# A graph attention kernel: one chunk of source rows in every eighth quad is loaded row by row by SyncE, and node inputs are loaded at the start of a quad's sums

## Chip, cores and metric

The kernel runs on one core of one Trainium2 chip. The metric is the device time of one execution in microseconds; the time before is the median of three runs. Five engines work side by side and wait for each other through semaphores: TensorE (PE, its weight loads PEld), VectorE (DVE), ScalarE (ACT), GpSimd (POOL) and SyncE (SP). SyncE computes nothing here; its instruction queue issues most DMAs. Gathers, which read one table row per index, are issued by GpSimd.

## What is computed

One layer of graph attention over 12,500 nodes and 200,000 edges, the edges sorted by destination, added to its input:

```python
h = jnp.maximum(_layernorm(x, axis=-1), 0.0)
h = (h @ W_node.T).reshape(num_nodes, H, HD)           # H = 4 heads of HD = 32
e = (edge_features @ W_edge.T).reshape(num_edges, H, HD)
att = jnp.sum(jnp.concatenate([h[src], h[tgt], e], -1) * a, axis=-1)
att = jnp.where(att > 0, att, 0.2 * att)
m = jnp.maximum(segment_max(att, tgt), 0.0)
ex = jnp.exp(att - m[tgt])
denom = segment_sum(ex, tgt) + (num_edges - deg)[:, None] * jnp.exp(-m)
out = x + segment_sum((ex / denom[tgt])[:, :, None] * h[src], tgt)
```

(The function is written here with the same names and fewer lines.) What costs time is `h[src]`: for every edge the row of its source node must be fetched, in no order.

## The kernel before

**Tiling.** The edges are cut into 392 groups of 511 (`G`, `NE`; a 512th place carries the sum of the group before). A group is four chunks of 128 edges (`J = 4`, one edge per partition). Four groups make a quad (`QG = 4`), so there are 98 quads. Two to four quads make a softmax batch (`supers`; four in the middle).

**Node stage** (lines 307 to 448). Normalized nodes are multiplied by the weights; rows of 137 float32 (548 bytes: values, a count and the source's share of the logit) are stored to the DRAM tensor `table`, target shares to `side`. Meanwhile the first gathers fetch raw inputs.

**Edge stage** (lines 463 to 895). The program is in an order written out by hand (`manual_schedule`): each engine gets its instructions in the order in which the Python code issues them; `together` interleaves generators step by step. For quad q:

- `fetch(q)`: SyncE loads edge features `ea` and destinations `db` (`fetch_edges`, lines 302 and 304) and, in `fetch_windows`, a window of target shares `pw` and one of node inputs `xw` for each group (lines 502 and 505). The windows' addresses are loaded into SyncE's registers first (`windows`, line 486). GpSimd issues the quad's 16 gathers from `table` into the buffer `ga` (line 141), which holds eight quads (`QUADS`). `fetch(q + 2)` is called when the logits of q begin.
- `logits(q, i)` for each group: VectorE compares destinations with node numbers (`at`, line 536), TensorE multiplies (lines 542 and 545); `add_sources` (lines 557 and 559) adds the sources' share out of `ga`.
- `softmax(s)` for a batch: transposes, scans (lines 592 to 661).
- `sums(q)`: VectorE weighs the gathered rows (line 736) and makes the marks `hot` (line 749); TensorE sums (line 754). `complete_group` carries the last row of the group before into the next (lines 683 and 687), makes the last product (line 688) and copies the sums to `pt` (line 689). A group's slot in `ga` is free for another quad's gathers once these products are done.
- `divide(q)`: VectorE divides (line 776), adds the node input `xw` (line 780), and SyncE stores the four windows of results to `out` (line 783). Neighbouring windows overlap, so a store waits until the one before has landed.

In SyncE's queue an iteration in the middle reads: `ea`, `db`, `pw` four times, `xw` four times, four stores. `db` has two buffers, so its load waits until VectorE has read the older one. All of SyncE's DMAs share eight completion semaphores in turn; a DMA waits until the one eight places before it has landed.

Of the kernel before, what the change touches and what calls it, by code (L numbers as in the profile page):

```python
# [8 lines left out]
F32 = mybir.dt.float32  # L9
BF16 = mybir.dt.bfloat16  # L10
I32 = mybir.dt.int32
AF = mybir.ActivationFunctionType
OP = mybir.AluOpType
AX = mybir.AxisListType

P = 128
H, HD = 4, 32
HW = HD + 1
D = H * HD
# [5 lines left out]
R_CNT, R_SRC, ROW = H * HW, H * HW + 1, H * HW + 5  # L25

J = 4
GE = J * P
NE = GE - 1
WIN = 96  # L30
SPAN = 92
QG = 4
# [4 lines left out]
AT_ONCE = 4  # L37
RAW, MORE = 4, 2
QUADS = 8
SETS = max(NODE_T, QG * J)  # L40
PAD = 1 << 20

# [6 lines left out]
def kernel(  # L49
# [35 lines left out]
    nc = tc.nc  # L85
# [8 lines left out]
    table = dram.tile([NP, ROW], F32, name="table")  # L94
# [27 lines left out]
    quads = blocks(G, QG)  # L122
    nq = len(quads)
# [4 lines left out]

    ga_all = consts.tile([P, QUADS, QG, J, ROW], F32, name="ga")
    GA, GATHERED = {}, set()  # L130

    def gather(q, rows, width, lo, hi):

        g0, m = quads[q]
        ga = GA[q] = ga_all[:, q % QUADS]
        for i in range(lo, hi):
            n = -(-min(E - (g0 + i) * NE + 1, GE) // P)
            if n < J:
                nc.vector.memset(ga[:, i, n:, :], 0.0)
            for j in range(n):  # L140
                nc.gpsimd.indirect_dma_start(  # L141
                    out=ga[:, i, j, 0:width], out_offset=None, in_=rows,
                    in_offset=bass.IndirectOffsetOnAxis(ap=srci[:, g0 + i, j:j + 1], axis=0))

    def held_gather(q, i, rows, width):

        nc.vector.memset(ga_all[0:1, q % QUADS, i, 0, 0:1], 0.0)
        gather(q, rows, width, i, i + 1)
# [8 lines left out]
    with tc.manual_schedule():  # L157
# [6 lines left out]
        for _ in range(AT_ONCE):  # L164
            q, i = early.pop(0)
# [12 lines left out]
        with tc.tile_pool(name="prep", bufs=1) as prep, tc.tile_pool(  # L178
            name="prep_ps", bufs=1, space=bass.MemoryType.PSUM
# [21 lines left out]
        def statistics(pool, rows, T):  # L201


            assert nc.vector.BN_STATS_DIM == 6
            stats = pool.tile([P, SETS, 6], F32, name="stats")
            for t in range(T):
# [3 lines left out]
            two = stats[:, :T, :].rearrange("p t (o k) -> p t o k", k=3)  # L210
            both = pool.tile([P, SETS, 2], F32, name="both")
            nc.vector.tensor_tensor(both[:, :T, :], two[:, :, 0, 1:3], two[:, :, 1, 1:3], op=OP.add)
            apart = pool.tile([P, SETS], F32, name="apart")
            nc.vector.tensor_tensor(apart[:, :T], two[:, :, 0, 1], two[:, :, 1, 1], op=OP.subtract)
# [92 lines left out]
        with tc.tile_pool(name="node", bufs=2) as node, tc.tile_pool(  # L307
            name="node_ps", bufs=2, space=bass.MemoryType.PSUM
        ) as node_ps, tc.tile_pool(name="index", bufs=1) as index, tc.tile_pool(
            name="index_ps", bufs=1, space=bass.MemoryType.PSUM  # L310
# [152 lines left out]
    with tc.tile_pool(name="work", bufs=2) as work, \  # L463
            tc.tile_pool(name="turned", bufs=1) as turned, \
            tc.tile_pool(name="ps", bufs=1, space=bass.MemoryType.PSUM) as ps:
        XW, LG, AT, U, DR = {}, {}, {}, {}, {}
# [17 lines left out]
        def windows(of, size, g, n):  # L484

            return nc.values_load_multi_w_load_instructions(
                of[0:1, g:g + n], engines=[mybir.EngineType.SP], min_val=0, max_val=(N - 1) * size,
                skip_runtime_bounds_check_because="a destination's row, and that is a node")[1]

        as_bytes = lambda d: d.bitcast(U8)  # L490
        rows_at = lambda d, at, size, rows=SPAN: as_bytes(d.rearrange("n c -> (n c)"))[
            bass.ds(at, rows * size)].rearrange("(n c) -> n c", c=size)
# [3 lines left out]
        def fetch_windows(q):  # L496
            g0, m = quads[q]
            pw = PW[q] = load.tile([SPAN, QG, SIDE], BF16, name="pw")
            xw = XW[q] = work.tile([WIN, QG, D], F32, name="xw", bufs=8)
            at = windows(base_side, 2 * SIDE, g0, m)  # L500
            for i in range(m):
                nc.sync.dma_start(as_bytes(pw[:, i, :]), rows_at(side, at[i], 2 * SIDE))
            at = windows(base_row, 4 * D, g0, m)
            for i in range(m):
                nc.sync.dma_start(as_bytes(xw[0:moved(q), i, :]), rows_at(x, at[i], 4 * D, moved(q)))
# [15 lines left out]
        def open_logits(q):  # L521
            if q == supers[of_quad[q]][0]:
                fetch_rows(of_quad[q])
            if q + 2 < nq:
                fetch(q + 2)
            AT[q] = work.tile([SPAN, QG, GE], BF16, name="at")
            LG[q] = ps.tile([P, QG, J, PIECES, H], F32, name="lg")
# [188 lines left out]

        def sums(q):

            g0, m = quads[q]
            s = of_quad[q]  # L720
            s0, sm = groups(s)
            ga = GA.pop(q)
            heads = lambda t: t[:, :, 0:sm * H].rearrange("p j (h g) -> p j h g", h=H)
            ex, xs, facs = XS[s]
            fc = facs[WIN:WIN + 1, 0:sm * H].rearrange("p (h g) -> p h g", h=H)
            pt = work.tile([WIN + 1, QG, ROW], F32, name="pt", bufs=3)
            hot = HOT.pop(q) if q in HOT else marks(q)
            beside = xs[:, :, 0:sm * (H + 1)].rearrange("p j (h g) -> p g j h", g=sm)
            nc.scalar.copy(ga[:, :m, :, R_CNT:R_SRC + H], beside[:, g0 - s0:g0 - s0 + m])

            def weigh(i):

                if i < m:
                    val = ga[:, i, :, 0:H * HW].rearrange("p j (h w) -> p j h w", w=HW)
                    weight = heads(ex)[:, :, :, g0 + i - s0]
                    nc.vector.tensor_tensor(  # L736
                        val, val, weight.unsqueeze(3).to_broadcast([P, J, H, HW]), op=OP.mult)

            ahead = 1 if q >= nq - 2 else 0
            for i in range(ahead):  # L740
                weigh(i)
            for i in range(m):
                g = g0 + i
                if q == nq - 1 - FREE and i == 1:
                    for k in range(FREE):
                        HOT[nq - FREE + k] = marks(nq - FREE + k)
                weigh(i + ahead)
                if q < nq - FREE:
                    nc.vector.tensor_tensor(  # L749
                        hot[:, i, :, 0:WIN], lane_ps.unsqueeze(1).to_broadcast([P, J, WIN]),  # L750
                        slot[:, g, :].unsqueeze(2).to_broadcast([P, J, WIN]), op=OP.is_equal)
                acc = ps.tile([P, 512], F32, name="acc", bufs=3)[0:WIN + 1, 0:ROW]
                for j in range(1, J):
                    nc.tensor.matmul(acc, hot[:, i, j, :], ga[:, i, j, :], start=j == 1, stop=False)  # L754
                complete()
                begun.append((q, i, ga, hot, pt, acc, fc[:, :, g - s0]))
                yield

        def divide(q, pt, den, lo, hi):

            n, R = hi - lo, moved(q)
            xw = XW[q][0:R, lo:hi]
            pt = pt[0:R, lo:hi]
            den = den[:, lo:hi]
            others = work.tile([WIN, QG], F32, name="others")[0:R]
            nc.vector.tensor_scalar(others[:, :n], pt[:, :, R_CNT], -1.0, float(E),
                                    op0=OP.mult, op1=OP.add)
            nc.vector.tensor_tensor(den, den, others[:, :n].unsqueeze(2).to_broadcast([R, n, H]),
                                    op=OP.mult)
            val = pt[:, :, 0:H * HW].rearrange("p g (h w) -> p g h w", w=HW)  # L770
            nc.vector.tensor_tensor(den, den, val[:, :, :, HD], op=OP.add)
            nc.vector.reciprocal(share_ps[0:R, :n, :], den)  # L772
            if not lo:
                RES[q] = work.tile([WIN, QG, D], F32, name="res")[0:R]
            res = RES[q][:, lo:hi]
            nc.vector.tensor_tensor(  # L776
                res[:, :n, :].rearrange("p g (h d) -> p g h d", d=HD), val[:, :, :, 0:HD],
                share_ps[0:R, :n, :].unsqueeze(3).to_broadcast([R, n, H, HD]), op=OP.mult)
            add = nc.gpsimd if q == nq - 2 or q == nq - 3 and lo else nc.vector
            add.tensor_tensor(res[:, :n, :], res[:, :n, :], xw, op=OP.add)  # L780
            at = windows(base_row, 4 * D, quads[q][0] + lo, n)
            for i in range(n):
                nc.sync.dma_start(rows_at(out, at[i], 4 * D, R), as_bytes(res[:, i, :]))

        def all_logits(q):
            flush()
            open_logits(q)
            for i in range(QG):
                logits(q, i)
                yield  # L790
            state["logits"] = q
# [51 lines left out]
        with tc.manual_schedule():  # L843
# [4 lines left out]

            held = [(q, i) for q in range(raw, min(QUADS, nq)) for i in range(raws(q), quads[q][1])]
            GATHERED.update(range(raw, QUADS))  # L850

# [241 lines left out]
```

## Time and profile before

| what | value |
|---|---|
| median of three runs | 2580.49 us (2579.14 to 2584.17) |
| the profiled execution | 2560.06 us, span of its instructions 2558.3 us |
| TensorE busy | 1425.0 us (56%) |
| VectorE busy | 1370.2 us (54%) |
| ScalarE busy | 403.5 us (16%) |
| GpSimd busy | 1507.2 us (59%) |
| mean granted TensorE clock | 0.526 |
| DMA | 297 MB in 195,917 packets, 116 GB/s |

The busy time of an engine is the union of its instructions; issuing a DMA, waiting and register work are not counted, so SyncE has no row. GpSimd's instruction for a gather counts as busy while it writes the transfer's descriptors; the data move afterwards. "Remote" as a releaser means that the profile saw the semaphore change but no instruction whose end fits the time of the change. The end of a matmul is modelled.

### The profile page before, as it was taken

How to read it: one execution, taken by the hardware profiler on the slowest of the kernel's cores; microseconds unless marked ns; L12 is line 12 of the kernel's file. 1: busy time of each engine (PE TensorE's matmuls, PEld its weight loads, DVE VectorE, ACT ScalarE, POOL GpSimd, SP SyncE). 2: the span in 40 equal slices, each digit the busy share in tenths (PEclk: the TensorE clock that was granted, in tenths of full speed). 3: DMA queues.
4: the chain of work that ended last, by engine and by line, in shares of the span. 5: the costliest groups of instructions: out<-in, count | busy, mean ns of one | idle time of the engine just before them, and what ended most of it. 6: DMA issues, size and time to landing. Idle time of an engine off the chain costs nothing. (4 is left out here: it accounts for less than half of the span.)

```text
span 2558.3 us, 27296 instructions
## 1 busy us (share of the span) xinstructions
PE 1425.0 (56%) x7317; PEld 1265.1 (49%) x7317; DVE 1370.2 (54%) x3362; ACT 403.5 (16%) x1531; POOL 1507.2 (59%) x1609
## 2 busy tenths in 40 slices
PE   4555645555555555555555555555655655655486
PEld 3544545544544445445545544544544544544475
DVE  4543545554554555555555555554554554555587
ACT  4533211111111111111111111111111110111112
POOL 6445546566666666566666666666666666666602
PEclk9665655555555555555555555555555555555556
DMA  5433354444445454444444444444444444434330
GB/s 181 153 111 97 99 133 122 109 119 125 113 119 129 108 132 121 106 125 117 117 125 117 116 124 117 116 121 121 116 120 112 123 114 120 123 100 119 94 94 17
DMA packets 195917, 297.27 MB, mean 116 GB/s; under 512 B 70633, under 2 KB 143593, under 8 KB 186354
## 3 DMA queue, kind: packets, MB, share of 16 engines
q1 hardware_dynamic: 143952, 183.30, 26.2%
q0 software_dynamic: 50112, 109.61, 17.4%
q10 hardware_dynamic: 1698, 2.58, 0.3%
q8 instruction: 61, 1.00, 0.2%
q14 instruction: 94, 0.77, 0.1%
HBM read 269.63 MB, written 25.73 MB: 115 GB/s over the span
## 5 line engine op out<-in xcount | busy, mean ns | idle before, releaser
L141 POOL DMA_INDIRECT ga<-table,srci x1494 | 1418.7, 950 | 903.9 <-issue 400.2
L754 PE MATMUL acc<-ga,hot 128*97 128x137 f32 x2352 | 647.6, 447 | 263.6 <-ACT hot L709 100.5
L754 PEld LDWEIGHTS acc<-ga,hot 128*97 128x97 f32 x2352 | 515.9, 278 | 287.3 <-ACT hot L709 101.9
L683 DVE TENSOR_TENSOR ga<-acc,facs 1x132 f32<-1x132 f32 x391 | 115.9, 296 | 710.7 <-ACT pt L689 597.9
L688 PE MATMUL acc<-ga,hot 128*97 128x137 f32 x784 | 267.7, 444 | 361.0 <-ACT ga L687 315.8
L545 PE MATMUL lg<-wblk,ea 128*128 128x8 f32 x1568 | 409.4, 359 | 0.0
L688 PEld LDWEIGHTS acc<-ga,hot 128*97 128x97 f32 x784 | 188.4, 277 | 396.7 <-ACT ga L687 342.3
L545 PEld LDWEIGHTS lg<-wblk,ea 128*128 128x128 f32 x1568 | 381.8, 309 | 0.0
L689 ACT COPY pt<-acc 97x137 f32<-97x137 f32 x392 | 107.1, 273 | 1529.1 <-remote 942.1
L542 PEld LDWEIGHTS <-at 92*128 92x128 bf16 x1568 | 213.9, 165 | 231.5 <-DVE at L536 95.8
L736 DVE TENSOR_TENSOR ga<-ga,ex_ps 128x528 f32<-128x528 f32 x392 | 268.7, 686 | 28.0 <-remote 27.7
L536 DVE TENSOR_TENSOR at<-const_ps,db 92x512 bf16<-92x512 f32 x392 | 267.3, 683 | 5.8
L542 PE MATMUL lg<-pw,at 92*128 92x12 bf16 x1568 | 170.6, 182 | 166.5 <-DVE at L536 80.1
L749 DVE TENSOR_TENSOR hot<-const_ps,slot 128x384 f32<-128x384 f32 x384 | 209.2, 545 | 0.0
L646 PE MATMUL ex_ps<-ident,ex 64*128 64x64 f32 (+2 forms) x112 | 18.6, 315 | 164.0 <-ACT ex L635 99.8
L646 PEld LDWEIGHTS ex_ps<-ident,ex 64*128 64x128 f32 (+2 forms) x112 | 13.8, 208 | 167.1 <-ACT ex L635 102.1
L141 POOL DMA_INDIRECT ga<-in_x_dram,srci x72 | 68.6, 952 | 43.6 <-issue 20.2
L687 ACT COPY ga<-acc 1x1 f32<-1x1 f32 x391 | 59.9, 153 | 189.5 <-DVE ga L683 113.7
L557 DVE TENSOR_REDUCE st<-lg 128x64 f32<-128x192 f32 x98 | 35.0, 357 | 87.9 <-remote 37.6
L395 PE MATMUL row_ps<-wcat,hT 128*128 128x137 f32 x198 | 45.7, 389 | 52.1 <-issue 15.6
L776 DVE TENSOR_TENSOR res<-pt,const_ps 92x512 f32<-92x512 f32 (+3 forms) x102 | 67.5, 662 | 4.4 <-issue 0.6
L780 DVE TENSOR_TENSOR res<-res,xw 92x512 f32<-92x512 f32 (+2 forms) x99 | 67.4, 681 | 3.4
(137 smaller groups left out, 1067.6 us busy)
## 6 DMA issues: line engine op xcount, KB each, us to landing
db<-in_dst_dram SPq DMA_DIRECT2D x98, 768.0 KB
ea<-in_edge_t_dram SPq DMA_DIRECT2D x98, 512.0 KB
ga<-table,srci POOLq DMA_INDIRECT x1494
xw<-in_x_dram SPq DMA_DIRECT2D x384, 46.0 KB
out_dram<-res SPq DMA_DIRECT2D x384, 46.0 KB
pw<-side SPq DMA_DIRECT2D x392, 2.2 KB
table<-row SPq DMA_DIRECT2D x9, 616.5 KB
xt<-in_x_dram SPq DMA_DIRECT2D x9, 576.0 KB
```

Of the source, the lines that this page charges most:

```text
L141: nc.gpsimd.indirect_dma_start(out=ga[:, i, j, 0:width], out_offset=None, in_=rows, in_offset=bass.IndirectOffsetOnAxis(ap=srci[:, g0 + i, ...
L536: nc.vector.tensor_tensor(at[:, i, :], node_ps[0:SPAN, g0 + i:g0 + i + 1].to_broadcast([SPAN, GE]), db[0:SPAN, i, :], op=OP.is_equal)
L542: nc.tensor.matmul(lg[:, i, j].rearrange("p k h -> p (k h)"), at[:, i, j * P:(j + 1) * P], sw, start=i + j == 0, stop=False, skip_group_ch ...
L545: nc.tensor.matmul(lg[:, i, 2 * w:2 * w + 2, 0, :], ea[:, i, w, :], wblk, start=False, stop=True, skip_group_check=True)
L683: nc.vector.tensor_tensor(ga[0:1, i, 0, 0:H * HW].rearrange("p (h w) -> p h w", w=HW), before[WIN:WIN + 1, 0:H * HW].rearrange("p (h w) -> ...
L688: nc.tensor.matmul(acc, hot[:, i, 0, :], ga[:, i, 0, :], start=False, stop=True)
L689: nc.scalar.copy(pt[:, i, :], acc)
L736: nc.vector.tensor_tensor(val, val, weight.unsqueeze(3).to_broadcast([P, J, H, HW]), op=OP.mult)
L749: nc.vector.tensor_tensor(hot[:, i, :, 0:WIN], lane_ps.unsqueeze(1).to_broadcast([P, J, WIN]), slot[:, g, :].unsqueeze(2).to_broadcast([P, ...
L754: nc.tensor.matmul(acc, hot[:, i, j, :], ga[:, i, j, :], start=j == 1, stop=False)
L776: nc.vector.tensor_tensor(res[:, :n, :].rearrange("p g (h d) -> p g h d", d=HD), val[:, :, :, 0:HD], share_ps[0:R, :n, :].unsqueeze(3).to_ ...
L780: add.tensor_tensor(res[:, :n, :], res[:, :n, :], xw, op=OP.add)
```

## The change

In 11 quads (16, 24, 32 … 96) the last chunk of the last group is no longer gathered: the loop over chunks in `gather` runs one step less. Its 128 rows are loaded by SyncE, each by a DMA of 548 bytes into a tile `rows`, with 16 row addresses at a time read into registers. The generator `by_rows` issues four of these DMAs at each step, and `divide` takes one step after each store. When the logits of such a quad begin, ScalarE copies `rows` into the quad's place in `ga`. The indices come by a small DMA and are turned into byte offsets by one VectorE instruction for each such quad. Apart from this, `xw` is loaded in a function of its own, `fetch_inputs`, called at the start of `sums(q)`, where it was loaded with `pw`, and has three buffers instead of eight.

```diff
+AHEAD, EVERY = 16, 8
...
+    whole = lambda g: E - g * NE + 1 >= GE
+    BY_ROW = {q: QG - 1 for q in range(AHEAD, nq, EVERY)
+              if quads[q][1] == QG and whole(quads[q][0] + QG - 1)}
...
-            for j in range(n):
+            for j in range(n - (q in BY_ROW and i == BY_ROW[q])):
                 nc.gpsimd.indirect_dma_start(
...
         def fetch_windows(q):
             g0, m = quads[q]
             pw = PW[q] = load.tile([SPAN, QG, SIDE], BF16, name="pw")
-            xw = XW[q] = work.tile([WIN, QG, D], F32, name="xw", bufs=8)
             at = windows(base_side, 2 * SIDE, g0, m)
             for i in range(m):
                 nc.sync.dma_start(as_bytes(pw[:, i, :]), rows_at(side, at[i], 2 * SIDE))
+
+        def fetch_inputs(q):
+            g0, m = quads[q]
+            xw = XW[q] = work.tile([WIN, QG, D], F32, name="xw", bufs=3)
             at = windows(base_row, 4 * D, g0, m)
             for i in range(m):
                 nc.sync.dma_start(as_bytes(xw[0:moved(q), i, :]), rows_at(x, at[i], 4 * D, moved(q)))
...
         def sums(q):
 
+            fetch_inputs(q)
             g0, m = quads[q]
...
+        def by_rows():
+
+            prepared = []
+
+            def prepare(q):
+                g = quads[q][0] + BY_ROW[q]
+                of = work.tile([1, P], I32, name="of")
+                nc.sync.dma_start(of, src.rearrange("(o e) -> o e", o=1)[
+                    :, (g + 1) * GE - P:(g + 1) * GE])
+                return of
+
+            nodes = sorted(BY_ROW)
+            of = prepare(nodes[0])
+            yield 0
+            for k, q in enumerate(nodes):
+                at_row = work.tile([1, P], I32, name="at_row")
+                nc.vector.tensor_scalar(at_row, of, float(4 * ROW), None, op0=OP.mult)
+                rows = ROWS[q] = work.tile([P, ROW], F32, name="rows")
+                for p0 in range(0, P, QG * QG):
+                    if p0 == P // 2 and k + 1 < len(nodes):
+                        of = prepare(nodes[k + 1])
+                    at = windows(at_row, 4 * ROW, p0, QG * QG)
+                    for p in range(QG * QG):
+                        nc.sync.dma_start(as_bytes(rows[p0 + p:p0 + p + 1, :]),
+                                          rows_at(table, at[p], 4 * ROW, 1))
+                        if p % QG == QG - 1:
+                            yield 0
+
+        ROWS, row_steps = {}, by_rows()
+        next(row_steps)
...
                 nc.sync.dma_start(rows_at(out, at[i], 4 * D, R), as_bytes(res[:, i, :]))
+                next(row_steps, None)
 
         def all_logits(q):
             flush()
             open_logits(q)
+            if q in BY_ROW:
+                nc.scalar.copy(GA[q][:, BY_ROW[q], J - 1, :], ROWS.pop(q))
```

## The prediction

> **What bounds the kernel now.** I read the page's groups first, then the time-ordered instructions of GpSimd, ScalarE and TensorE, then SyncE's waits. A group line shows count and shapes, then busy us and mean ns, then idle us before it and what ended it.
>
> ```profile
> L141 POOL DMA_INDIRECT ga<-table,srci x1494 | 1418.7, 950 | 903.9 <-issue 400.2 <-remote 258.2 <-PE acc L688 162.9
> L689 ACT COPY pt<-acc 97x137 f32<-97x137 f32 x392 | 107.1, 273 | 1529.1 <-remote 942.1
> ```
>
> No engine is over 59% busy, so shares decide nothing. The gathers idle 400 us in 0.30 us steps between neighbours (1.25 us from one to the next) and some 420 us waiting for TensorE to free a buffer. That last looks as if TensorE, not GpSimd, were the limit. The order of time says otherwise (start us, duration us, idle before and releaser in brackets):
>
> ```profile
> 1248.23 0.94 POOL L141 DMA_INDIRECT ga<-table,srci  x1 [2.46 <-remote]
> 1249.47 0.94 POOL L141 DMA_INDIRECT ga<-table,srci  x1 [0.30 <-issue]
> ...
> 1261.96 0.94 POOL L141 DMA_INDIRECT ga<-table,srci  x1 [0.30 <-issue]
> 1265.63 0.94 POOL L141 DMA_INDIRECT ga<-table,srci  x1 [2.73 <-remote]
> ```
>
> ```profile
> 1257.66 0.78 PE L688 MATMUL acc<-ga,hot 128*97 128x137 f32 x2 [0.30 <-issue]
> 1266.24 0.77 PE L688 MATMUL acc<-ga,hot 128*97 128x137 f32 x2 [5.29 <-ACT ga L687]
> ```
>
> ```profile
> 1257.45 0.15 ACT L687 COPY ga<-acc 1x1 f32<-1x1 f32 x1 [0.36 <-issue]
> 1265.40 0.27 ACT L689 COPY pt<-acc 97x137 f32<-97x137 f32 x1 [7.79 <-remote]
> ```
>
> GpSimd runs twelve gathers, three groups, then stops. TensorE finished a group's sum at 1258.44; the copy waiting for it began at 1265.40, only 2.5 us after GpSimd's run ended at 1262.90. The next group's L688 stood behind that copy. So TensorE's signal reaches nobody while gathers run, and everything moves on after GpSimd has stopped for want of a buffer. The pattern repeats: run starts at 1345.00, 1362.40, 1379.68, 1396.93, 1414.45, 1424.12, 1441.46. Sixteen groups take 96.5 us: 64 gathers at 1.25 us (80 us) and six pauses of 2.4 to 5.0 us. The pauses follow the runs, so the rate is GpSimd's.
>
> The second witness is the end, where the gathers are over (last start 2435.4). The chain of waits has:
>
> ```profile
> 2451.60 1.18 DVE run L601
> 2485.17 1.18 DVE run L601
> ```
>
> That is one softmax to the next, two quads: 16.8 us a quad, although these short softmax batches cost more per quad than the middle's batches of four. With gathers a quad takes 96.5/4 = 24.1 us. The consumers could go faster; GpSimd's runs hold them.
>
> SyncE is the queue that gets the work. Its waits (us in all, times, longest):
>
> ```profile
> SPq L304 <- DVE at L536: 394.4, 44, 22.2
> SPq L783 <- DMA out_dram<-res: 218.2, 164, 2.8
> ```
>
> and a stretch of its queue:
>
> ```profile
> 1247.90 6.04 SPq L783 DMA_DIRECT2D out_dram<-res  x4
> 1254.04 0.38 SPq L302 DMA_DIRECT2D ea<-in_edge_t_dram  x1
> 1266.74 0.34 SPq L304 DMA_DIRECT2D db<-in_dst_dram  x1
> ...
> 1271.28 4.94 SPq L505 DMA_DIRECT2D xw<-in_x_dram  x4
> ...
> 1317.52 1.40 SPq L505 DMA_DIRECT2D xw<-in_x_dram  x4
> ```
>
> SyncE idles before `db`, and between the stores of one quad, each waiting for the one before to land. Its issues come at two paces: the same four take 1.40 us or 4.94 us (0.35 or 1.24 each), the latter late in a gather run.
>
> **The change, part by part.**
>
> *Eleven gathers go* (quads 16, 24 … 96; GpSimd's stream falls from 1494 to 1483). Each is 0.945 + 0.30 = 1.25 us. Where do they fall? Counting gathers in the trace, quad 48's last starts at 1256.96: eighth of the run 1248.23 to 1262.90, which then ends in a 2.73 us pause. Ten of the eleven stand like that, four before a pause called remote; quad 40's has eight behind it. So the run is eleven long, GpSimd stops 1.25 us earlier, and by the reading above the signal and all after it come 1.25 us earlier. 11 x 1.25 = 13.7 us off the path. Bounds: 0, if the pause only grows; and 11 x 24.1/16 = 16.6, if pauses shrink with the gathers. I take 13.7: the pauses show as fixed (2.36 to 2.73 after runs of twelve).
>
> *SyncE gets 1408 one-row loads of 548 bytes*, 16 per quad over 88 quads, four behind each store; 88 register loads, 11 index loads. At the short pace a row takes 0.35 us, four 1.4 us. The stores above start (6.04 - 0.25)/3 = 1.93 us apart, of which about 0.38 is work: 1.55 us of waiting, in which four rows hide. Three of four sets hide; the last (1.4 us) and a register load about every quad (0.5 us) do not: 1.9 us a quad. The cover is the `db` idle: 394 + 75 (the wait ended by DVE `col`) + 23 over 98 quads = 5.0 us a quad. Cost taken: 0. Without any cover it would be 88 x 1.9 = 167 us. At the long pace the four take 5 us, so one set in four at that pace adds about (5.0 - 1.6) = 3.4 us a quad; 5.3 against 5.0 is near the edge, but the next item gives some back, and a delay is not at once a loss: quad 48's `db` went out at 1266.74 and its first reader, L536, ran at 1292.8, and other quads show 25 to 38 us. What is issued late is `ea`, `db`, `pw` and the stores; their readers L536 and L542 come an iteration later, and `res` has two buffers.
>
> *Node inputs move* from behind `pw`, where four issues took 4.94, 4.97, 1.40 and 4.19 us in successive quads, to the start of the quad's sums, right behind the previous stores and rows. No DMA is added; at the short pace it is 1.4 us plus the register load. That returns up to 2.5 us of SyncE time a quad, off the path. New is a wait: the add L780 now needs `xw` loaded about one iteration (some 20 us) before, formerly many. Behind L780 on VectorE stand the next L536, L736 and L749, and TensorE behind them. A load issued within 15 us is in time. Cost 0; if SyncE falls behind by an iteration it is the saturation rival.
>
> *Copies and indices.* Eleven ScalarE copies of 128x137: between L729 (128x80, 0.33) and L661 (128x256, 0.37), so 0.35 each, 3.9 us in all; ScalarE is 16% busy and waits before L689 (942 us). They wait for eight DMA lanes, whose last row was stored behind a quad two iterations earlier; L594, L687 and L689 queue behind. Eleven VectorE multiplications of 1x128 at most 0.30 (L683, 1x132): 3.3 us, right behind a finished `res`. Taken as 0, together at most 7 us.
>
> *The tail.* Quad 97's `xw` is now issued between the last stores, about 1.9 us of SyncE. Before, L780 of that quad ran at 2548.5 and the store ahead at 2543.25, so it lands with a microsecond to spare: 0.5 us.
>
> Sum: -13.7 + 0.5 = -13.2. On the profiled span of 2558.3 (execution 2560.06) that gives 2545. The runs' median is 20.4 us above that execution; I subtract the same: 2580.5 - 13.2 = 2567.
>
> The Trainium skill (DMA: Bandwidth & Descriptors, Rules for kernel authors) speaks against this change: many small transfers should be merged, since below 64 KB one pays mostly overhead. If every row cost a landing, as a chained store does here, the result is the saturation rival below. The four `xw` issues in 1.40 us show independent loads not waiting for each other.
>
> **Rivals.**
>
> *SyncE saturates (slower).* Place: rows behind stores, at the long pace. SyncE has 5.0 us of `db` idle and 3 x 1.55 = 4.6 us between stores, 9.6 us a quad; 16 rows and 0.5 of register load use it up at 0.57 us a row. From there on each 0.1 us a row costs 1.6 us x 88 = 141 us. At 0.63 us (one row in three at the long pace): 0.06 x 16 x 88 = 84, less 13: 2651. If all waited for landings, 1.93 a row: 1.36 x 16 x 88 = 1915 more. For: the long pace exists and begins near these DMAs. Against: `xw` leaves it, and stores mostly come just after the release.
>
> *The pauses lengthen (slower).* The added issues and completions travel where TensorE's signals are stuck, and a pause grows by one row set's share, say the 0.35 us of one issue per quad: 88 x 0.35 = 31, so 2598. For: SyncE and TensorE are held up together. Against: 1408 packets beside 143,952 of that queue are 1%.
>
> *No gain.* The consumers need the time anyway, the pause grows by what GpSimd saves: 2580. For: GpSimd is released by TensorE. Against: 16.8 us a quad without gathers.
>
> *It doesn't do what it says:* excluded, the emitted order shows 1483 gathers.
>
> **How the numbers follow.** Forecast (2562 to 2571) 0.60; pauses lengthen 0.15; SyncE saturates 0.13; no gain 0.12. Predicted 2567. Its own range 2560 to 2573. For eight in ten: down to 2555 (16.6 saved, and some runs' spread, 2579 to 2584), up to 2606, which takes in no gain and most of the lengthened pauses and leaves saturation out. This kernel's measurement tells about 0.2% (5 us) from no change. Faster 0.61 (forecast and a sliver), same 0.12, slower 0.27.
>
> **What would show it.** Right: runs of eleven gathers in quads 16, 24 …, the pause behind them still 2.4 to 2.7 us, two softmax batches there in about 191.7 us, not 193; `db` idle smaller but present; L780 without a DMA wait. Wrong: `db` idle gone and `ea` late for L545; L780 released by `xw`; L689's remote idle up by as much as GpSimd saved.

## The result and the profile after

| | before | after |
|---|---|---|
| median | 2577.7 us (6 runs, 2570.57 to 2584.17) | 2691.01 us (6 runs, 2680.74 to 2718.28) |
| ratio, 95% interval | | 1.0455, 1.04 to 1.0511 |
| profiled execution | 2560.06 us, span 2558.3 | 2718.28 us, span 2716.5 |

The kernel became 113 us slower by the medians; 2567 had been forecast, with a range up to 2606. The profiled execution of the changed kernel is the longest of its six, so single sums of its trace are 1% large; the two traces lie 158 us apart, not 113.

The groups of the changed kernel, in the columns of the prediction's first fence (the add of node inputs, L780 before, is now L819; it had sat idle 3.4 us in all):

```profile
L145 POOL DMA_INDIRECT ga<-table,srci x1483 | 1417.3, 956 | 1054.8 <-issue 401.8
...
L696 ACT COPY pt<-acc 97x137 f32<-97x137 f32 x392 | 107.4, 274 | 1313.1 <-remote 723.2
...
L819 DVE TENSOR_TENSOR res<-res,xw 92x512 f32<-92x512 f32 (+2 forms) x99 | 67.1, 677 | 346.9 <-DMA xw<-in_x_dram 317.5
```

Eleven gathers are gone, yet GpSimd idles 151 us more than before (903.9). ScalarE's copy waits less for "remote" than before (942.1). The new wait is the third line. The waits of all engines say what GpSimd waits for (us in all, times, longest):

```profile
POOL ga L145 <- PE acc L695: 372.1, 75, 23.7
...
DVE res L819 <- DMA xw<-in_x_dram: 317.5, 58, 12.3
...
POOL ga L145 <- remote: 193.5, 87, 3.4
```

The same two waits of GpSimd were 162.9 us (36 times) and 260.3 us (105 times) before. The remote pauses have not lengthened: 2.22 us each against 2.48. What grew is waiting for a real product that comes late. Counting a run of gathers as ended by a gap of more than 0.6 us, 107 runs had 12 gathers and 14 had 8 before; now 39 have 12 and 103 have 8.

SyncE's own waits:

```profile
SPq L308 <- DVE at L543: 73.6, 11, 22.4
SPq L822 <- DMA out_dram<-res: 71.3, 74, 3.8
```

Before, these were 394.4 and 218.2 us. The idle time that was to cover the rows is used up: from the start of `ea`'s issue to the start of `db`'s was 7.79 us on the mean over the 98 quads before, and is 1.63 now. A stretch of SyncE's queue (start us, us from the first issue's start to the last one's end, line, transfer, count):

```profile
1302.12 0.32 SPq L822 DMA_DIRECT2D out_dram<-res  x1
1303.79 1.67 SPq L790 DMA_DIRECT2D rows<-table  x4
1306.44 0.29 SPq L822 DMA_DIRECT2D out_dram<-res  x1
1307.12 3.62 SPq L790 DMA_DIRECT2D rows<-table  x4
1310.83 0.62 SPq L822 DMA_DIRECT2D out_dram<-res  x1
1312.27 6.41 SPq L790 DMA_DIRECT2D rows<-table  x4
1319.38 0.01 SPq L822 DMA_DIRECT2D out_dram<-res  x1
1319.48 1.19 SPq L790 DMA_DIRECT2D rows<-table  x4
1321.41 1.41 SPq L512 DMA_DIRECT2D xw<-in_x_dram  x4
1322.91 0.37 SPq L306 DMA_DIRECT2D ea<-in_edge_t_dram  x1
1323.38 0.37 SPq L308 DMA_DIRECT2D db<-in_dst_dram  x1
```

The first and last of the four stores begin 17.3 us apart; over all quads in the middle the median is 14.2 us, before 5.9. Only then can `xw` go out, at 1321.41, and `db` follows `ea` at once. What comes of it, in the order of time, first on VectorE, then TensorE, then GpSimd (in brackets the idle time before and its releaser):

```profile
1320.66 0.68 DVE L815 TENSOR_TENSOR res<-pt,const_ps 92x512 f32<-92x512 f32 x1 [7.57 <-DMA rows<-table]
1327.28 0.69 DVE L819 TENSOR_TENSOR res<-res,xw 92x512 f32<-92x512 f32 x1 [5.94 <-DMA xw<-in_x_dram]
...
1328.03 0.67 DVE L543 TENSOR_TENSOR at<-const_ps,db 92x512 bf16<-92x512 f32 x1
```

```profile
1328.75 0.22 PE L549 MATMUL lg<-pw,at 92*128 92x12 bf16 x2 [15.63 <-DVE at L543]
...
1331.31 0.66 PE L695 MATMUL acc<-ga,hot 128*97 128x137 f32 x2
```

```profile
1323.63 0.94 POOL L145 DMA_INDIRECT ga<-table,srci  x1 [0.30 <-issue]
1332.24 0.95 POOL L145 DMA_INDIRECT ga<-table,srci  x1 [7.67 <-PE acc L695]
```

This is one chain: the add stands 5.94 us for `xw`, the comparison L543 runs only behind it in VectorE's order, TensorE has stood 15.63 us for that comparison, the group's last product L695 ends at 1331.97, and GpSimd goes on 0.27 us later after 7.67 us without work. (L815's releaser is named as a row load; that instruction waits for four semaphores, and the `res` it writes is freed by stores. The name is the profile's inference.)

The end is as it was. The chain of waits has two scans of the softmax 33.56 us apart, as before:

```profile
2607.55 1.18 DVE run L608
...
2641.11 1.18 DVE run L608
```

From the last gather's start to the end of the span it was 122.9 us and is 125.2 us. The loss lies in the middle.

### The profile page after: what moved, and what is told of

It is laid out like the page before. It is cut to its first block, busy times and chain, and to the rows that moved or that the text cites. A ratio compares the mean times of both kernels' runs of the same rounds, so it can differ in the third digit from the quotient of the medians.

```text
span 2716.5 us, 30468 instructions
## 1 busy us (share of the span) xinstructions
PE 1405.4 (52%) x7317; PEld 1265.4 (47%) x7317; DVE 1370.6 (50%) x3373; ACT 408.7 (15%) x1542; POOL 1506.3 (55%) x1598
## 5 line engine op out<-in xcount | busy, mean ns | idle before, releaser
L549 PEld LDWEIGHTS <-at 92*128 92x128 bf16 x1568 | 220.1, 167 | 603.6 <-DVE at L543 446.4
L695 PE MATMUL acc<-ga,hot 128*97 128x137 f32 x784 | 263.4, 439 | 205.7 <-ACT ga L694 136.5
L695 PEld LDWEIGHTS acc<-ga,hot 128*97 128x97 f32 x784 | 192.7, 279 | 226.5 <-ACT ga L694 147.7
L543 DVE TENSOR_TENSOR at<-const_ps,db 92x512 bf16<-92x512 f32 x392 | 267.2, 682 | 6.0
L819 DVE TENSOR_TENSOR res<-res,xw 92x512 f32<-92x512 f32 (+2 forms) x99 | 67.1, 677 | 346.9 <-DMA xw<-in_x_dram 317.5
L815 DVE TENSOR_TENSOR res<-pt,const_ps 92x512 f32<-92x512 f32 (+3 forms) x102 | 67.5, 662 | 82.6 <-DMA out_dram<-res 42.5
L399 PEld LDWEIGHTS row_ps<-wcat,hT 128*128 128x128 f32 x198 | 37.1, 266 | 67.7 <-ACT hn L233 28.6
L663 PE MATMUL acc<-ident,run 64*128 64x64 f32 (+2 forms) x112 | 18.8, 317 | 90.7 <-ACT facs L660 73.7
```

Source lines behind the costliest of these rows:

```text
L399: nc.tensor.matmul(row_ps[:, t, :ROW], hT[:, t, :], wcat, start=True, stop=True)
L543: nc.vector.tensor_tensor(at[:, i, :], node_ps[0:SPAN, g0 + i:g0 + i + 1].to_broadcast([SPAN, GE]), db[0:SPAN, i, :], op=OP.is_equal)
L549: nc.tensor.matmul(lg[:, i, j].rearrange("p k h -> p (k h)"), at[:, i, j * P:(j + 1) * P], sw, start=i + j == 0, stop=False, skip_group_ch ...
L695: nc.tensor.matmul(acc, hot[:, i, 0, :], ga[:, i, 0, :], start=False, stop=True)
L815: nc.vector.tensor_tensor(res[:, :n, :].rearrange("p g (h d) -> p g h d", d=HD), val[:, :, :, 0:HD], share_ps[0:R, :n, :].unsqueeze(3).to_ ...
```

## Experiments

The runs were made on three chips, and each ratio is against runs of the kernel before on the same chip. Before took 2017.86 us on the first (7 runs), 2577.77 us on the second (17) and 2557.69 us on the third (17); the second and third are of the kind on which the change was first measured. Differences in us are worked out from the ratios. In the expectations, theory S is that SyncE's time to issue sets the pace (the saturation rival), rival L is that inputs loaded late do the harm, and rival P that the pauses of the gathers lengthen; other letters are told where they are used.

### First chip: parts of the change alone

**Inputs late, no rows, all gathers.**

```diff
-    BY_ROW = {q: QG - 1 for q in range(AHEAD, nq, EVERY) ...}
+    BY_ROW = {}
-        ROWS, row_steps = {}, by_rows()
-        next(row_steps)
+        ROWS, row_steps = {}, iter(())
```

> Only the move of the node inputs: loaded at the start of the sums with three buffers, all gathers kept, no rows. Theory S (SyncE's issuing time now sets the pace, because of the rows): no change, 2578 within 0.5%, db idle on SyncE still 4 to 5 us a quad. Rival L (the inputs come too late and hold VectorE at the add): a good part of the 113 us shows here too, 2620 or more, with waits of the add on the load of xw.

2027.96 us, ratio 1.005 (1.0033 to 1.0067). The moved inputs cost 10 us on this chip, a tenth of what the change costs on the other. The add did wait for `xw`, 102.9 us in 31 pieces, so L's wait exists here without any row; the same kernel on the third chip, below, shows no such wait.

**Rows, inputs early** (`fetch_inputs` called in `fetch`, eight buffers; to make room, rows and their addresses share a tile with `node_at`).

```diff
-    node_at = consts.tile([P, G], F32, name="node_at")
+    node_all = consts.tile([P, 2 * ROW + 2 * P], F32, name="node_at")
+    node_at = node_all[:, 0:G]
...
-            xw = XW[q] = work.tile([WIN, QG, D], F32, name="xw", bufs=3)
+            xw = XW[q] = work.tile([WIN, QG, D], F32, name="xw", bufs=8)
...
             fetch_windows(q)
+            fetch_inputs(q)
...
-            fetch_inputs(q)
             g0, m = quads[q]
             s = of_quad[q]
...
-                of = work.tile([1, P], I32, name="of")
+                k = nodes.index(q) % 2
+                of = node_all[0:1, 2 * ROW + k * P:2 * ROW + (k + 1) * P].bitcast(I32)
...
-                at_row = work.tile([1, P], I32, name="at_row")
+                at_row = of
-                rows = ROWS[q] = work.tile([P, ROW], F32, name="rows")
+                rows = ROWS[q] = node_all[:, k % 2 * ROW:(k % 2 + 1) * ROW]
```

> Rows by SyncE and eleven gathers fewer, but the inputs loaded two quads ahead with eight buffers as before the change. S: SyncE has as much to issue as in the changed kernel, so about as slow, 2660 to 2700, and something else than xw is late (db, ea, pw or res). L: the harm is gone, 2564 to 2578. Rival P (rows lengthen GpSimd's pauses): slow, but with idle time of SyncE before db left.

2209.83 us, ratio 1.0951 (1.0921 to 1.098). With the inputs early the loss is not gone, so L is not the whole of it. But this kernel turned out to be no clean copy of the change, as its instructions by line show (count, then ns: least, median, most, then first and last start in us):

```profile
L791 SPq MOVE node_at<-table x1408: 29/29/37, 172.8 to 2073.1; - x176
L791 SPq DMA_DIRECT2D node_at<-table x1408: 227/228/332, 172.9 to 2073.1; - x176
```

```profile
L491 SPq TENSOR_LOAD <-base_row x200: 278/572/947, 101.1 to 2200.9; - x100
...
L491 SPq TENSOR_LOAD <-node_at x88: 3436/3536/3699, 169.3 to 2062.7; - x88
```

The rows are quick here (0.34 us from one to the next), and the register load of 16 addresses takes 3.54 us; in the changed kernel's trace it took 1.24. Eighty-eight times 2.3 us are 202 us, about as much as this kernel lost (192 us). So its size says nothing of the change's, and an aligned version follows on the second chip. What is late here are the divisions: by the profile VectorE waited 274.9 us for stores and 252.2 us for row loads before L816. SyncE also has less idle time on this chip: from the start of `ea`'s issue to that of `db`'s it was 2.89 us a quad in the first experiment, and is 0.90 here.

**No rows, eleven gathers fewer, inputs early** (ScalarE copies ones in place of rows, so the sums of 11 chunks are not the reference's).

```diff
-        ROWS, row_steps = {}, by_rows()
-        next(row_steps)
+        ROWS, row_steps = {q: ones[:, 0:1].to_broadcast([P, ROW]) for q in BY_ROW}, iter(())
```

(and `fetch_inputs` in `fetch` with eight buffers, as above)

> Eleven gathers fewer and no rows loaded: the place in ga gets ones by the same ScalarE copy, inputs early as before the change; the sums of 11 chunks are therefore not the reference's. All theories share the prediction's first term: 11 x 1.25 = 13.7 us less, 2564. If GpSimd's rate does not set the pace: 2578.

2006.23 us, ratio 0.9938 (0.9922 to 0.9955): -12.5 us. The gathers' term stands, -13.7 forecast.

**Rows loaded and not used, all gathers kept, inputs early.**

```diff
-            for j in range(n - (q in BY_ROW and i == BY_ROW[q])):
+            for j in range(n):
...
-            if q in BY_ROW:
-                nc.scalar.copy(GA[q][:, BY_ROW[q], J - 1, :], ROWS.pop(q))
```

(the rest as in the second kernel)

> Rows loaded by SyncE but not used, all gathers kept, inputs early: the cost of the 1408 loads by themselves. S: as e2, at most 14 us more, 2660 to 2715. L: no change, 2578. P: as e2 plus 14 us, SyncE not saturated.

2208.07 us, ratio 1.0941 (1.0911 to 1.0971), the same as with eleven gathers fewer. The loss needs neither the copy nor the missing gathers, and where SyncE is the bound the gathers saved do not show.

### Second chip: the change itself, aligned, halved, without addresses

**The changed kernel as it is.**

> The changed kernel as it is, beside the versions with early inputs and on whatever chip these four share. Theory S (SyncE's issue time is the bound): the ratio to before stays above 1.03; SyncE's register loads of 16 addresses show 1.24 us as in the first trace of this kernel and rows 0.34 us apart where the chip does not hold them back. Rival A (the harm of +9.5% in e2 and e5 came from their own register loads, 3.54 us each instead of 1.24, because the address tile lay at 1096 bytes, not at a multiple of 64): if this chip is like that of the first four experiments, this kernel is far below theirs, within about 1% of before. Rival C (the +4.5% belongs to the chip of the first pair, where signals are held back and rows go 0.75 us apart): ratio 1.00 to 1.01 on a chip where before takes 2018 us, 1.045 on one where it takes 2578 us.

2689.78 us, ratio 1.0431 (1.0413 to 1.0449), as in the first pair, and as S and C both had it for a chip of this kind. What the change does where before takes 2018 us was not measured, so A and the other half of C stay open for that chip.

**Inputs early, addresses at a multiple of 64 bytes in the shared tile.**

```diff
-                of = node_all[0:1, 2 * ROW + k * P:2 * ROW + (k + 1) * P].bitcast(I32)
+                of = node_all[0:1, k * P:(k + 1) * P].bitcast(I32)
...
-                rows = ROWS[q] = node_all[:, k % 2 * ROW:(k % 2 + 1) * ROW]
+                rows = ROWS[q] = node_all[:, 2 * P + k % 2 * ROW:2 * P + (k % 2 + 1) * ROW]
```

(against the second kernel above)

> As e2_rows_inputs_early, with the address rows at a multiple of 64 bytes in the tile they share. Rival A: the load of 16 addresses goes from 3.54 to 1.24 us, 88 times, so 202 us of SyncE's time go, and with them most of e2's 192 us: ratio 0.99 to 1.01. Theory S without A: the load stays at 3.5 us or the time stays near 2200 us though it shortens: ratio above 1.05.

2638.93 us, ratio 1.0248 (1.0235 to 1.0262). Its loads of 16 addresses are back at 1.20 us, but on this chip A's forecast of 0.99 to 1.01 fails, and so does S's of more than 1.05: most of the harm stays, though it is 0.0183 (47 us) less than with late inputs. Where the wait went is in its groups:

```profile
L816 DVE TENSOR_TENSOR res<-pt,const_ps 92x512 f32<-92x512 f32 (+3 forms) x102 | 67.6, 662 | 286.8 <-DMA out_dram<-res 145.6
...
L820 DVE TENSOR_TENSOR res<-res,xw 92x512 f32<-92x512 f32 (+2 forms) x99 | 67.0, 677 | 3.4
```

The add no longer waits for inputs; now the division before it waits 286.8 us, of which the profile puts 145.6 down to stores, which free `res`, and 81.2 to row loads. Late inputs are one of two ways in which a late SyncE reaches VectorE.

**Half as many rows in a quad** (inputs late).

```diff
-AHEAD, EVERY = 16, 8
+AHEAD, EVERY = 24, 16
...
-                        if p % QG == QG - 1:
+                        if p % 2 == 1:
                             yield 0
```

> Half as many rows in a quad (a chunk in every sixteenth quad, two rows behind a store; inputs late as in the changed kernel; 5 gathers fewer instead of 11). Theory S: SyncE gets back about 3.5 us a quad and the harm falls by more than half, to a ratio below 1.02. If the harm came from the late inputs alone it stays as large as in the changed kernel.

2558.06 us, ratio 0.9928 (0.9911 to 0.9945). The harm doesn't halve, it vanishes, as the threshold of the saturation rival would have it. Late inputs, which this kernel keeps, are not the cause by themselves.

**Rows from fixed addresses** (16 transfers a quad as in the change, no register load and no MOVE before a transfer; the sums of 11 chunks are taken from other rows than the reference's).

```diff
-                    at = windows(at_row, 4 * ROW, p0, QG * QG)
+                    at = [4 * ROW * (p0 + p) for p in range(QG * QG)]
```

> The changed kernel with 16 row transfers in a quad as before, but from fixed addresses: no register load of addresses and no MOVE ahead of a transfer (the sums of 11 chunks are taken from other rows than the reference's). It sizes what the addresses cost. Theory S with rows at 0.34 us: 1.3 us of load and 16 x 0.06 us of MOVE a quad go, so the ratio falls by at most 0.04 and some harm stays. If the register loads are the term that decides, the ratio goes to 1.00 or below.

2564.63 us, ratio 0.9959 (0.9943 to 0.9974). The same 1408 transfers on the same queue, and the kernel is below before, -10.6 us by the ratio where -13.2 had been forecast for the change. Against the change on the same chip that is 0.0472 of ratio: some 122 us hang on how a transfer gets its address. The line's instructions (ns: least, median, most), first here and then in the changed kernel's first trace:

```profile
L790 SPq DMA_DIRECT2D rows<-table x1408: 2/251/3448, 256.7 to 2431.0; - x176
```

```profile
L790 SPq MOVE rows<-table x1408: 2/29/1397, 264.5 to 2573.8; - x176
L790 SPq DMA_DIRECT2D rows<-table x1408: 2/228/2274, 264.5 to 2573.9; - x176
```

A MOVE, which puts an address in place, is 29 ns at the median and up to 1397. From a MOVE's start to the next instruction it was 0.335 us on the mean in the changed kernel's first trace, from a transfer's 0.415: 471 us of SyncE's time in MOVEs alone. On the first chip no MOVE took over 37 ns.

### Third chip: load or MOVE, and the parts again

**One address loaded for 16 transfers** (MOVEs kept; the sums of 11 chunks are taken from other rows than the reference's).

```diff
-                    at = windows(at_row, 4 * ROW, p0, QG * QG)
+                    at = windows(at_row, 4 * ROW, p0, 1) * (QG * QG)
```

> The changed kernel, but of 16 addresses only the first is loaded and serves all 16 transfers, so the register load is shorter and the MOVE ahead of every transfer stays (the sums of 11 chunks are taken from other rows than the reference's). It divides what fixed addresses took off (1.0431 against 0.9959, 122 us, where before takes 2578 us). Theory M (the MOVEs: in the changed kernel's trace a MOVE took 0.2 to 0.4 us to the next instruction on the mean, 1408 of them some 420 us of SyncE's time, partly hidden): the ratio stays above 1.025. Theory R (the register load of 16 addresses, 1.24 us, 88 of them 109 us): the ratio falls below 1.01. On a chip where before takes 2018 us no more can be said than their order.

2647.61 us, ratio 1.0334 (1.0312 to 1.0356). The load fell from 1.24 to 0.56 us, the MOVEs stayed, and so did most of the harm: M, not R. The shorter load is worth 0.0097 (25 us), against the change on the second chip.

**Inputs late alone, again** (edit as in the first).

> Only the node inputs moved, all gathers, no rows: on a chip where before takes 2018 us it was 1.005. Where before takes 2578 us: 1.000 to 1.005 if the move costs what it did there; 0.994 or less if it returns SyncE's time ahead of the gathers, as half the rows ended 19.7 us below before with only five gathers fewer, 6.3 us.

2554.75 us, ratio 0.9991 (0.9974 to 1.0007). Neither harm nor gain can be told here.

**Inputs late, eleven gathers fewer, no rows** (ones copied in place of rows, so the sums of 11 chunks are not the reference's; the edit of `ROWS, row_steps` shown above, inputs left as in the changed kernel).

> The changed kernel without the rows and their addresses: inputs late, eleven gathers fewer, the copy of ScalarE kept (it copies ones, so the sums of 11 chunks are not the reference's). The gathers' term alone is -13.7 us; with the inputs' move on top 0.990 to 1.000. Under theory S all of the harm goes with the rows; if it stays above 1.02, the harm is in the moved inputs or the copies. The difference from e7_fixed_rows (0.9959) is what 1408 transfers cost without their addresses.

2540.63 us, ratio 0.994 (0.9917 to 0.9963): -15.3 us, the gathers' term on a chip of the second kind, with the moved inputs in place. The copies stay in it and do no harm.

**Half as many rows, inputs early and aligned** (`AHEAD, EVERY = 32, 16`, two rows behind a store, otherwise the aligned version).

> Half as many rows in a quad, inputs early with eight buffers as in the kernel before, five gathers fewer. If late inputs cost by themselves, this is below e4_half (0.9928 where before takes 2578 us): about 0.990. If moving them had helped, it is above: 0.997 to 1.000.

2533.08 us, ratio 0.9894 (0.987 to 0.9917): below the kernel before, -27 us by the ratio. It is the fastest version by ratio that computes the whole layer, but its interval overlaps with that of half the rows with late inputs (0.9911 to 0.9945), which ran on another chip, and the gain stays near 1%.

### The runs side by side

All are from chips on which before takes some 2570 us. "Slack" is the mean time from the start of `ea`'s issue to that of `db`'s (0.4 to 0.5 us is the issue itself), the next column VectorE's wait for `xw`, the last GpSimd's wait for a group's last product. Each line is of one profiled execution; that of the kernel with fixed addresses ("+ 1408 transfers") is the longest of its twelve.

| kernel | ratio | slack, us a quad | `xw` wait, us | GpSimd's wait, us |
|---|---|---|---|---|
| before | 1 | 7.79 | none listed | 162.9 |
| inputs late | 0.9991 | 8.41 | none listed | 159.8 |
| + 11 gathers fewer, copies | 0.9940 | 8.28 | none listed | 159.3 |
| + 1408 transfers | 0.9959 | 3.90 | 50.7 | 177.6 |
| + MOVEs, short load | 1.0334 | 1.70 | 277.3 | 319.0 |
| + load of 16 (the change) | 1.0431 | 1.80 | 268.1 | 339.2 |
| change, inputs early | 1.0248 | 1.57 | none listed | 280.6 |
| half the rows, inputs late | 0.9928 | 5.12 | 28.3 | 150.3 |
| half the rows, inputs early | 0.9894 | 5.10 | none listed | 156.8 |

Read downwards, the first six rows build the change up. As long as slack is left, each step costs next to nothing; the step that uses it up, the MOVEs with a short load, costs 0.0375, some 97 us (its two runs were on two chips). The 1408 transfers alone cost 0.0019, some 5 us, with intervals that overlap and on two chips. The three kernels with slack below 2 us are slower than before, all with 3.9 or more are not. The slack is one store that all parts draw on: the transfers took 4.4 us of it and cost nearly nothing, the MOVEs and the short load took the next 2.2 and cost the time, and half as many rows with their MOVEs cost nothing. So which part "made" the loss depends on the order in which they are added.

## Why the prediction was wrong

**The step that failed** is SyncE's 1408 row loads, "Cost taken: 0". Everything else in the sum held or was too small to matter, and the mechanism in its place is the one that the prediction set down as its saturation rival with a chance of 0.13. Three sizes in the step were off:

- *The pace of a row.* It was priced at the short pace, 0.35 us, and with one set in four at the long one; that case already asked 5.3 us of a cover of 5.0, and the cost was still taken as 0. Measured from row to row within a set, the changed kernel took 0.75 us on the mean, 52% of the steps over 0.6. The reading "late in a gather run" was right: of the steps that began in the first 2.5 us of a run of gathers 28% were over 0.6 us, between 2.5 and 5 us 65%, later 88%, and outside the runs 37%. How many sets would fall there was wrong: the stores no longer came together just after a release, as the prediction held, but spread over 14 us. The run from 1303.56 to 1317.0 in the stretch above held two sets at the long pace, those at 1307.12 and 1312.27, and the prediction's own `xw` sets (4.94, 4.97, 1.40 and 4.19 us) were at it in three of four.
- *What a row is.* The prediction read the four `xw` issues as four instructions. They are eight: a MOVE and a transfer each. Its 0.35 and 1.24 us, taken from issue to issue, held the MOVEs already, so this did not change its price; it hid a part that can be taken away. At the short pace the MOVE is 0.06 us of the 0.34 from row to row; over the whole changed kernel it takes 0.335 us to the next instruction, a transfer 0.415. It is not only these two that go slow: in the stretch above a MOVE took 0.698 us (at 1310.03), a transfer 0.696 (at 1312.27) and a wait for a semaphore 0.697 (at 1318.68). Without MOVE and load the transfers came 0.53 us apart, just inside the 0.57 that the prediction gave as the point where the cover is used up, and the loss was gone. This was shown by taking the address away.
- *The register load* of 16 addresses was set at 0.5 us, the duration of loads of four. It took 1.24. By the run with one address, cutting it to 0.56 us is worth 25 us.

A quad thus asked SyncE for 16 x 0.75 + 1.25 = 13.3 us where the prediction reckoned 16 x 0.35 + 0.5 = 6.1 and knew of 9.6 us of cover.

The Trainium skill (Runtime: NRT & Kernel Launch, Instruction fetch mechanics) puts a register load at about 200 ns a register, said of loads that the runtime makes from HBM; taken over to these loads from a tile, 16 addresses would take an estimated 3.2 us. The runs hold both: 3.54 us in the second kernel, 1.24 us in the change. That figure would have pointed to the load; the runs give the MOVEs, with a load of one address, the greater share. The Trainium skill's rule on small transfers (DMA: Bandwidth & Descriptors, Rules for kernel authors), which the prediction weighed, had the right sign, yet 1408 small transfers from fixed addresses cost next to nothing here.

**The other points.**

- *Eleven gathers, -13.7*: right in size, -12.5 us on the first chip and -15.3 (-21 to -9.5) on the third. The picture behind it held in part. In the run without rows on the third chip only two of the eleven quads have a run of eleven with a pause of 2.5 us behind it; the others have runs of seven or three with pauses of 1.0 to 1.9 us. On the first chip there are no such pauses (843 gathers in one run), and the saving is the same. The time of the gathers is what both share.
- *Node inputs, cost 0*: right by themselves, 0.9991 and 1.005. Wrong in company: "in time within 15 us" did not hold once stores were spread over 14 us, and with SyncE late the early inputs are 47 us better. The prediction had said that this would then be the saturation rival, and it is.
- *Copies and indices, 0*: right within what the run without rows tells. The eleven copies took 305 ns each, 0.35 forecast.
- *Tail, 0.5*: 2.3 us by the two traces; with moved inputs and no rows at all the stretch is 125.1 us too, with early inputs and half the rows 122.9 us. That points to the moved inputs, but early inputs with all rows show 124.4, so it is not settled.
- *Pauses lengthen*: no. They were fewer and shorter (193.5 us in 87 against 260.3 in 105).
- *No gain* from fewer gathers: no, by the two runs without rows.
- *Saturation*: right in place, in its sign and in what it shows (`db` idle gone, the add released by `xw`), and too steep in price. By its rule, each 0.1 us a row above 0.57 costs 141 us, the 0.75 us and the longer load would have cost some (13.3 - 9.6) x 88 = 326 us; 113 and the gathers' 14 are some 127. The slack of the loads themselves, which the prediction had put at 25 to 38 us before the first reader of `db`, fell to 10 to 24 us and took a part; how much is not shown.

**What stays open.** Half the rows gained 18.6 and 27 us with five gathers fewer, for which 6.3 us are due. No run shows where the rest comes from. Why instructions on SyncE go at the long pace was not tried either; that MOVEs, transfers and semaphore waits go slow alike, mostly while gathers run, is what the traces show. Every time here comes with a recorded span, so no run tells whether the recording of SyncE's instructions takes part in that pace. The run with one address, which tells MOVEs from load, was on another chip than the two runs it is compared with, and it kept a load of one address; the MOVEs alone were not priced.

## What to carry to other kernels

Count a queue's instructions, not its transfers: a transfer with an address from a register brings a MOVE and a share of a register load, and here the same transfers without these cost nothing that the runs can tell, with them some 4%. When work is put into a queue's idle time, price it at the longer pace seen in the same trace, add up what one iteration holds, and keep the margin: at half the load the same idea gained about 1%, at the full load it lost 4.5%. And look for the second way in which a late queue is felt; moving the inputs back early won 47 us and left the rest of the loss in a wait for the stores.

## What the runs showed of the hardware

- The same kernel took 2018 us on one chip and 2558 to 2578 us on two others. The remote pauses and SyncE's long pace are on the latter only: over 1408 MOVEs the longest was 37 ns on the first chip and 1.1 to 1.4 us on the others, in kernels with the same 16 rows in a quad. On the slower ones the long pace goes with the gathers: in the changed kernel's first trace 88% of the steps from row to row that began over 5 us into a run of gathers took more than 0.6 us, in the second kernel on the first chip 1%.
- A register load of 16 addresses took 3.54 us at the median in one tile and 1.20 to 1.24 us in others, in kernels with 16 rows in a quad (0.69 in the last kernel, with half of them and early inputs), while loads of four row addresses took 0.55 to 0.58 us everywhere. The long ones began 1096 bytes into their tile, not at a multiple of 64, but were also the only ones on the first chip, so place and chip are not told apart.
